# Keys and values of a cross attention by seven products of halved blocks instead of eight

## The chip, the cores and the metric

The kernel runs on one core of a Trainium2 chip. Its metric is the device time of one execution in microseconds (us). The matrix engine is TensorE (PE); VectorE (DVE), ScalarE (ACT) and GpSimd (POOL) work beside it, and SyncE (SP) issues most of the transfers. All arithmetic here is in 32-bit floating point.

## The reference, cut to what matters

Two decoder layers work on 8 entries of 256 tokens of width 256. The change lies in the cross attention of the second layer, 16 heads of 64 with one learned key and value ("null") in front. The context of an entry is 256 tokens of width 512:

```
q = split_heads(x @ Wq)                        # [256, 256] @ [256, 1024]
k, v = split(context @ Wkv)                    # [256, 512] @ [512, 2 x 1024]
k, v = concat(null_k, k), concat(null_v, v)
out = softmax(q k^T / 8) v @ Wout              # heads joined, [256, 1024] @ [1024, 256]
x = x + layernorm(out) * ln_scale + ln_bias
```

A feed-forward layer with a shared expert (weights ws1, ws3, ws2) and eight routed experts follows.

## The kernel before

The tiles live in pools; a pool with `bufs=n` gives a name n buffers in turn, and a new use waits until the old one is read. A scheduler orders the instructions of each engine at build time, except where a manual order is declared; each engine then works its own queue from front to back, waiting for semaphores. PE is in manual order in the last entry of the cross attention and after it.

`product` (L272 to L274) is the matmul helper of nearly everything here: it gives one product as two matmuls, one for each 64 columns of the 128 stationary columns. The profile lists each 32-bit matmul as two records, each with its own weight load, so `product` shows as four records.

`null_cross_attention` (L1043) handles the entries b = 0 to 7 in turn. The loop body begins with `weighted(kT, v, qT)` of entry b, which makes the scores (stx, L1100), their exponentials (pTx, ACT, L1104), a sum of the two key halves (both, POOL, L1106), the products with the values (ox, L1138) and, by a matmul with a table of ones, the denominators (den, L1114). Scores of two pairs of heads run ahead; both has four buffers. Then come the layer norm of entry b+1 (`layernorm_T`, transposes tr), the norm and routing scores of entry b-1 for the expert layer (`routed_norm`, `routed_rows`, `routed_scores`: xne, sc), and `reciprocals`, which turns the denominators round, sends them to memory and reads them back spread over partitions (rd, rs). While that transfer is under way PE makes the keys and values of entry b+1:

- `keys(b + 1)` loads the transposed context (ctxT, two buffers) and calls `features` with the key half of wkv_x: 4 groups of 16 matmuls with 256 moving columns (fm, 64 matmuls), each group copied out of the accumulation banks by ACT;
- `vals(ctxT)` makes the values: 4 groups of 8 matmuls with 512 moving columns (vps), each copied by ACT.

After that `divide` multiplies the output by rs (L1186; half on DVE, half on POOL), `outward(b, ...)` multiplies by Wout (wo) and normalizes the result with DVE and POOL (lxrs L256, yx L1203 and L1204, x L1205), and `queries(xnT)` makes the scores of the null key (nps) and the queries of entry b+1 (fm with wq_x, 32 matmuls, four copies on DVE). Then the next entry's `weighted` begins.

The accumulation banks: pool mm has three banks in turn for fm, vps, ox, wo, tr, sc and nps; pool scp has two tiles of two banks for the scores; den has its own. Tag pT has four buffers.

`load_shared` (L920) loads the router and the three matrices of the shared expert once, before the loop, into a pool of their own (L914). In the last entry `wproj.close()` frees the context weights, and the pool "mids" takes their place.

Of the kernel before, what the change touches and what calls it, by code (L numbers as in the profile page):

```python
# [28 lines left out]
F32 = mybir.dt.float32  # L29
# [4 lines left out]
ALU = mybir.AluOpType  # L34
# [4 lines left out]
P = 128  # L39
B, S, D = 8, 256, 256  # L40
# [3 lines left out]
CTX = 512  # L44
XH, XD = 16, 64
# [4 lines left out]
NFC = len(FCH)  # L50
# [105 lines left out]
def plain(  # L156
# [4 lines left out]
    nc = tc.nc  # L161
# [100 lines left out]
    def layernorm_T(b, work, mm):  # L262

        xn = work.tile([P, 2, D], F32, tag="xn", name="xn")
        mv, rs = norm_stats([x[:, 2 * b + t, :] for t in range(2)], 1e-5, small, "ln")
        for t in range(2):
            last = normed(xn[:, t, :], x[:, 2 * b + t, :], mv, rs, t)
        return last, transposed(xn, work, mm, "xnT")
# [3 lines left out]
    def product(out, lhsT, rhs, start, stop):  # L272
        for h in (slice(0, 64), slice(64, P)):
            nc.tensor.matmul(out[h], lhsT[:, h], rhs, start=start, stop=stop, skip_group_check=True)  # L274
# [481 lines left out]
    nc8 = XH // 2  # L756
# [139 lines left out]
    def w_in(pool, src1, src3, name):  # L896

        t = pool.tile([P, 2, 2 * FF + tail], F32, name=name, tag=name)
        nc.sync.dma_start(t[:, :, :FF], src1.rearrange("(c p) f -> p c f", p=P))
        nc.sync.dma_start(t[:, :, FF + tail :], src3.rearrange("(c p) f -> p c f", p=P))  # L900
        nc.gpsimd.tensor_copy(t[:, :, FF : FF + tail], t[:, :, 2 * FF :])
        return t

    def ended(t):

        nc.gpsimd.memset(t[tail:, full, :], 0.0)
        return t

    def w_out(t, src):
        nc.sync.dma_start(t[:, :full, :], src[: full * P].rearrange("(c p) d -> p c d", p=P))  # L910
        nc.sync.dma_start(t[:tail, full, :], src[full * P :])
        return t
# [4 lines left out]
    norms = [(const.tile([P, 2, 2], F32, name=f"mean{b}"), const.tile([P, 2], F32, name=f"rstd{b}")) for b in range(B)]  # L917
    shared = {}

    def load_shared():  # L920

        router = pool_s.tile([P, 2, E], F32, name="router")
        nc.gpsimd.dma_start(router, a["L1_ffn_router_DE"].rearrange("(c p) e -> p c e", p=P))
        xnT = pool_s.tile([P, 2, B * S], F32, name="xnTe")
        ws13 = w_in(pool_s, a["L1_ffn_ws1_DF"], a["L1_ffn_ws3_DF"], "ws13")
        ws2 = w_out(ended(pool_s.tile([P, NFC, D], F32, name="ws2")), a["L1_ffn_ws2_FD"])
        shared.update(router=router, xnT=xnT, ws13=ws13, ws2=ws2)

    def hidden(mid, first, n, pair, silu):

# [109 lines left out]

    def null_cross_attention(phase):  # L1043
        work = phase.enter_context(tc.tile_pool(name="d2", bufs=2))
        scale = XD**-0.5

        def features(dst, w, rows, copy):
            n = w.shape[1]
            for c2 in range(0, nc8, 2):
                ps = mm.tile([P, 2, S], F32, tag="mm", name="fm")  # L1050
                for i in range(2):
                    for cc in range(n):
                        product(
                            ps[:, i, :], w[:, cc, (c2 + i) * P : (c2 + i + 1) * P], rows[:, cc, :], cc == 0, cc == n - 1
                        )
                copy(dst[:, c2 : c2 + 2, :], ps)

        def keys(b):
            ctxT = ctxs.tile([P, CTX // P, S], F32, tag="ctxT", name="ctxT")
            nc.sync.dma_start(ctxT, a["ctx_T"][b].rearrange("(c p) t -> p c t", p=P))  # L1060
            kT = work.tile([P, nc8, S], F32, tag="kT", name="kTx", bufs=1)
            features(kT, wkv_x, ctxT, nc.scalar.copy)
            return ctxT, kT

        def vals(ctxT):
            v = work.tile([P, 2, XH, XD], F32, tag="vx", name="vx", bufs=1)
# [13 lines left out]
            return v  # L1080

        def queries(xnT):
            nps = mm.tile([P, 2, S], F32, tag="mm", name="nps")
            for k in range(2):
                product(nps[:, 0, :], wn[:, k].rearrange("p g w -> p (g w)"), xnT[:, k, :], k == 0, k == 1)
            qT = work.tile([P, nc8, S], F32, tag="qT", name="qTx", bufs=1)
            features(qT, wq_x, xnT, nc.vector.tensor_copy)
            en = work.tile([P, S], F32, tag="en", name="en")
            nc.scalar.activation(en, nps[:, 0, :], AF.Exp, scale=scale)
            return qT, en  # L1090

        def weighted(kT, v, qT):

# [57 lines left out]

        def reciprocals(b, den, en):

            r = work.tile([P, S], F32, tag="rx", name="rx")
            nc.vector.tensor_tensor(r, den, en, ALU.add)
            nc.vector.reciprocal(r, r)
            rd = dram.tile([2, nc8, S], F32, name=f"rd{b}")
            rs = work.tile([P, nc8, S], F32, tag="rs", name="rs", bufs=1)
            for g in range(2):
                nc.sync.dma_start(rd[g], r[XD * g : XD * g + nc8, :])  # L1160
            for g in range(2):
                nc.sync.dma_start(
                    rs[XD * g : XD * (g + 1)].rearrange("p c q -> p (c q)"),
                    rd[g : g + 1].rearrange("g c q -> g (c q)").to_broadcast([XD, nc8 * S]),
                )
            nc.gpsimd.tensor_tensor(en, en, r, ALU.mult)
            low = work.tile([P, S], F32, tag="low", name="low")
            nc.vector.tensor_scalar(low, r, 1.0e-25, None, ALU.is_ge)
            nc.vector.scalar_tensor_tensor(
                low, r, 1.0e25, low, ALU.is_le, ALU.mult, accum_out=fit[:, b : b + 1]  # L1170
            )
            return rs

        def in_range():

            for k in range(3):
                v = dens[:, k].rearrange("p t h -> p (t h)")
                low = work.tile([P, S], F32, tag="low", name="lowk")
                nc.vector.tensor_scalar(low, v, 1.0e-25, None, ALU.is_ge)
                nc.vector.scalar_tensor_tensor(  # L1180
                    low, v, 1.0e25, low, ALU.is_le, ALU.mult, accum_out=fit[:, B + k : B + k + 1]
                )
# [5 lines left out]
                )  # L1188

        def outward(b, oT, en):  # L1190
            y = work.tile([P, 2, D], F32, tag="y", name="yx")
            ps = mm.tile([P, 2, D], F32, tag="mm", name="wo")
            for t in range(2):
                cols = bass.ts(t, P)
                product(ps[:, t, :], en[:, cols], nvw, True, False)
                for c in range(nc8):
                    product(ps[:, t, :], oT[:, c, cols], wout_x[:, c, :], False, c == nc8 - 1)
            nc.scalar.copy(y, ps)  # L1198
            mv, rs = norm_stats([y[:, t, :] for t in range(2)], 1e-6, small, "lx")
            for t in range(2):  # L1200
                xt = x[:, 2 * b + t, :]
                normed(y[:, t, :], y[:, t, :], mv, rs, t)
                nc.gpsimd.tensor_tensor(y[:, t, :], y[:, t, :], lns, ALU.mult)  # L1203
                nc.gpsimd.tensor_tensor(y[:, t, :], y[:, t, :], lnb, ALU.add)  # L1204
                nc.gpsimd.tensor_tensor(xt, xt, y[:, t, :], ALU.add)  # L1205
# [10 lines left out]


        _, xnT = layernorm_T(0, work, mm)
        ctxT, kT = keys(0)
        v = vals(ctxT)  # L1220
        qT, en = queries(xnT)
        load_shared()
        order = ExitStack()
        for b in range(B):
            more = b + 1 < B
            oT, den = weighted(kT, v, qT)
            if more:
                _, xnT = layernorm_T(b + 1, work, mm)
            else:

                wproj.close()
                late = ctx.enter_context(tc.tile_pool(name="mids", bufs=1, side="right"))

                shared["mid_s"] = [ended(late.tile([P, NFC, 2 * S], F32, name=f"mid{i}")) for i in range(2)]
                routing_tables(late)
                order.enter_context(tc.manual_schedule(engines={mybir.EngineType.PE}))
            if b:
                routed_rows(b - 1, routed_norm(b - 1, work), work)
            rs, old = reciprocals(b, den, en), en
            if b == 1:  # L1240
                in_range()
            if more:
                ctxT, kT = keys(b + 1)
            if more:
                if b:
                    routed_scores(b - 1)
                v = vals(ctxT)
            else:
                for i, _ in enumerate(quarter(0)):
                    if i == 0:  # L1250
                        routed_scores(b - 1)
            divide(oT, rs)
            outward(b, oT, old)
            if more:
                qT, en = queries(xnT)
        order.close()
        with tc.manual_schedule(engines={mybir.EngineType.PE, mybir.EngineType.DVE}):
            for i, _ in enumerate(quarter(1)):
# [1228 lines left out]
```

## Time and profile before

| | |
|---|---|
| median of 3 runs | 1399.54 us (1398.04 to 1402.86) |
| profiled execution, its own time | 1396.5 us |
| its span | 1394.8 us |
| granted TensorE clock | 0.994 of full speed |
| PE busy | 1357.5 us, 97% of the span |
| keys of eight entries, fm<-ctxT,wkv_x | 112.9 us, 1024 records of 256 columns |
| values of eight entries, vps<-wkv_x,ctxT | 111.8 us, 512 records of 512 columns |
| queries of eight entries, fm<-xnT,wq_x | 57.0 us, 512 records |
| wo<-wout_x,oT | 58.0 us, 512 records |
| POOL both (L1106) | 79.6 us, 64 of 1273 ns |

Busy time of a group is the union of its records, so it is what the group takes of PE, while the mean length of one record includes its overlap with its neighbours. The span is the time between the first and last instruction that the profiler saw; the execution's own time is 1.7 us longer. In a timeline the columns are start (us from the start of the span), length, engine, source line, operation, tiles, shapes and count, and in brackets the idle time before it with what ended it.

### The profile page before, as it was taken

Reading aid. Unit: us, or ns where it says so; the run is one execution under the profiler, and the core shown is the slowest. Engines: PE = TensorE matmul, PEld = TensorE weight load, DVE = VectorE, ACT = ScalarE, POOL = GpSimd, SP = SyncE. Lnnn points to the kernel's source line nnn. Section 1 sums busy time; section 2 is a strip of 40 time slices with the busy share of each in tenths; the row PEclk is TensorE's granted clock in tenths of the full one; section 3 lists DMA queues with packets and bytes.
Section 4 is the critical chain, followed back from the end, with each engine's and each line's share of the span. In section 5 each row is a group of like instructions: output and inputs, shape, how many; then the busy total and the mean of one; then the engine's idle time right before and its main releaser. Section 6 shows DMA issues by size and latency. Waiting matters only on the chain.

```text
span 1394.8 us, 28640 instructions
## 1 busy us (share of the span) xinstructions
PE 1357.5 (97%) x12198; PEld 884.4 (63%) x12198; DVE 502.4 (36%) x1467; ACT 457.4 (33%) x730; POOL 395.7 (28%) x499
## 2 busy tenths in 40 slices
PE   6999999999999999989999999999999999999998
PEld 3666756756766666665655656565656555688884
DVE  5443563563565654330222213131312225422213
ACT  2555444444444434431222313131322222122221
POOL 4222142052033234220332415152423412400004
PEclk9999999999999999999999999999999999999999
DMA  8960000000000006010101010110101010779954
GB/s 312 345 205 16 9 24 9 8 24 1 1 9 2 2 9 221 1 53 26 32 16 31 16 47 2 46 32 16 32 1 32 1 31 5 283 289 414 402 209 127
DMA packets 46921, 116.56 MB, mean 84 GB/s; under 512 B 8273, under 2 KB 30401, under 8 KB 42433
## 3 DMA queue, kind: packets, MB, share of 16 engines
q1 hardware_dynamic: 38912, 92.74, 19.3%
q0 software_dynamic: 5152, 18.89, 3.6%
q10 hardware_dynamic: 2720, 3.02, 0.6%
q8 instruction: 98, 1.61, 0.5%
q14 instruction: 39, 0.31, 0.1%
HBM read 104.00 MB, written 27.93 MB: 95 GB/s over the span
## 4 chain that ended last, share of the span: by engine, by line
PE 85%; DVE 5%; POOL 4%; issue 1%; ACT 1%; DMA 0%; ACTq 0%; POOLq 0%; DVEq 0%; SPq 0%
PE fm L274 12%; PE st L332 9%; PE o L364 9%; PE vps L274 8%; PE h L274 6%; PE wo L274 4%; PE ox L1138 4%; PE stx L1100 4%; PE out L1475 3%; PE out L1292 3%; PE h L947 3%; PE qk L274 3%; PE hx L947 3%; PE tr L281 3%; PE den L1114 2%; PE ao L274 2%
## 5 line engine op out<-in xcount | busy, mean ns | idle before, releaser
L364 PE MATMUL o<-pT,padv 128*64 128x256 f32 (+1 forms) x1536 | 171.6, 365 | 1.1 <-POOL pT L344 1.1
L341 ACT ACTIVATE pT<-st 128x1024 f32<-128x1024 f32 (+1 forms) x128 | 110.5, 915 | 88.8 <-PE st L332 87.9
L364 PEld LDWEIGHTS o<-pT,padv 128*64 128x64 f32 x1536 | 103.1, 137 | 52.7 <-issue 10.0
L332 PE MATMUL st<-qm,kT 64*128 64x256 f32 (+1 forms) x1024 | 117.2, 367 | 0.9 <-DVE qm L310 0.6
L274 PE MATMUL fm<-ctxT,wkv_x 128*64 128x256 f32 x1024 | 112.9, 380 | 0.0
L274 PE MATMUL vps<-wkv_x,ctxT 128*64 128x512 f32 x512 | 111.8, 593 | 0.0
L332 PEld LDWEIGHTS st<-qm,kT 64*128 64x128 f32 x1024 | 90.1, 189 | 26.0 <-issue 15.6
L274 PEld LDWEIGHTS fm<-ctxT,wkv_x 128*64 128x64 f32 x1024 | 73.0, 137 | 37.3 <-issue 1.3
L1106 POOL TENSOR_TENSOR both<-pTx 128x512 f32<-128x512 f32 x64 | 79.6, 1273 | 57.4 <-ACT pTx L1104 33.8
L1104 ACT ACTIVATE pTx<-stx 128x1024 f32<-128x1024 f32 x64 | 62.1, 1021 | 89.9 <-PE stx L1100 86.8
L274 PE MATMUL h<-xrT,w 128*64 128x128 f32 (+1 forms) x1936 | 86.9, 250 | 1.4 <-issue 1.4
L274 PEld LDWEIGHTS h<-xrT,w 128*64 128x64 f32 x1936 | 84.3, 137 | 4.4 <-issue 2.1
L274 PEld LDWEIGHTS vps<-wkv_x,ctxT 128*64 128x64 f32 x512 | 36.4, 137 | 68.9 <-issue 68.6
L341 ACT ACTIVATE pT<-st,kbias 128x1024 f32<-128x1024 f32 x64 | 68.0, 1113 | 28.7 <-PE st L332 28.7
L256 POOL TENSOR_TENSOR lnrs<-lnve,mhalf 128x2 f32<-128x2 f32 x48 | 34.2, 717 | 147.0 <-DVE lnve L254 95.2
L332 PE MATMUL st<-qm,memk 64*128 64x256 f32 x512 | 68.8, 393 | 0.5
L939 ACT ACTIVATE sl<-h 128x128 f32<-128x128 f32 (+1 forms) x114 | 35.4, 310 | 96.1 <-PE h L274 56.7
L1100 PE MATMUL stx<-qTx,kTx 64*128 64x256 f32 x512 | 64.3, 391 | 2.5 <-ACT pTx L1104 2.5
L940 DVE TENSOR_TENSOR midr<-sl,h 128x128 f32<-128x128 f32 x102 | 29.4, 288 | 100.5 <-PE h L274 68.6
L251 DVE BATCH_NORM_STATS2 lxst<-yx 128x6 f32<-128x256 f32 x16 | 6.0, 418 | 162.7 <-ACT yx L1198 162.7
L274 PE MATMUL qk<-l_wqkv,xnT 128*64 128x512 f32 x256 | 62.6, 610 | 0.7 <-ACT xnT L284 0.7
L344 POOL TENSOR_SCALAR_AFFINE_SELECT pT<-pT 128x512 f32<-128x512 f32 x64 | 39.5, 638 | 83.1 <-ACT pT L341 79.8
(274 smaller groups left out, 2080.7 us busy)
## 6 DMA issues: line engine op xcount, KB each, us to landing
w<-packs SPq DMA_DIRECT2D x22, 1408.0 KB
w<-packs SPq DMA_DIRECT2D x22, 768.0 KB
rs<-rd SPq DMA_DIRECT2D x16, 512.0 KB
packs<-L_ffn_w_eDF SPq DMA_DIRECT2D x8, 704.0 KB
packs<-L_ffn_w_eDF SPq DMA_DIRECT2D x8, 640.0 KB
packs<-L_ffn_w_eFD SPq DMA_DIRECT2D x8, 640.0 KB
ctxT<-ctx_T SPq DMA_DIRECT2D x8, 512.0 KB
wkv_x<-L_xattn_Wkv POOLq DMA_DIRECT2D x1, 4096.0 KB, 17.3
```

The costliest lines, as they stand in the source:

```text
L274: nc.tensor.matmul(out[h], lhsT[:, h], rhs, start=start, stop=stop, skip_group_check=True)
L281: nc.tensor.transpose(ps[:, c, t * P : (t + 1) * P], rows[:, t, c * P : (c + 1) * P], ident)
L332: nc.tensor.matmul(st[:, g, i, :n], kT[rows, c, bass.ts(kt, P)], qm[rows, 2 * mq + i, c, q0:], start=True, stop=True,)
L341: nc.scalar.activation(pT[:, :, :, :n], st[:, :, :, :n], AF.Exp, scale=scale, **kb)
L364: nc.tensor.matmul(o[64 * i : 64 * i + 64, mq, q0:], v_pad[:, kt, 4 * c + 2 * mq + i, 2 * g : 2 * g + 2, :], pTs[kt][:, g, i, : S - q0], s ...
L947: nc.tensor.matmul(h, shared["ws13"][:, c, lo : lo + P], shared["xnT"][:, c, bass.ts(q, 2 * S)], start=c == 0, stop=c == 1)
L1100: nc.tensor.matmul(st[:, g, kt, :], kT[rows, c, bass.ts(kt, P)], qT[rows, c, :], start=True, stop=True)
L1104: nc.scalar.activation(pT, st, AF.Exp, scale=scale)
L1106: nc.gpsimd.tensor_tensor(both, pT[:, :, 0, :], pT[:, :, 1, :], ALU.add)
L1138: nc.tensor.matmul(o[XD * g : XD * (g + 1), i, :], v[:, kt, 2 * (c2 + i) + g, :], pT[:, g, kt, :], start=kt == 0, stop=kt == 1, skip_group ...
L1292: nc.tensor.matmul(ps, mid[:, i, lo : lo + P], w2[:, i, :], start=i == 0, stop=i == NFC - 1)
L1475: nc.tensor.matmul(ps[h], mid[:, i, h], sets[k % len(sets)][1][:, i, :], start=i == 0, stop=i == NFC - 1, skip_group_check=True,)
```

## The change

For entries 1 to 7 keys and values are made by the seven products of the Strassen-Winograd scheme. The product context times weights is cut into blocks: the tokens into two halves of 128, the 512 context features into two of 256, and the output columns into two of 512, for the keys and the values each. Four sums of weight blocks are made once (three in a new tile tw, the fourth in place of block (0, 1)); four sums of context blocks are made for every entry on DVE (three in sw, one in place). `seven` issues the products, the accumulating sums and the evacuations, and is a generator, so that keys and values alternate and a bank is read while PE fills another. Each product of the keys is 16 matmuls of 128 moving columns, each of the values 4 of 512. Entry 0 is made as before.

The queries of entry b+1 are moved ahead of `divide` and `outward` of entry b and are interleaved with the last products of the values. The null key's exponential follows its scores at once. The context is requested at the start of the loop body. To make room, the three matrices of the shared expert are loaded in the last entry, when the context weights are given up, and the tiles rx, low and y have one buffer instead of two.

```diff
-    def load_shared():
-        router = ...
-        ws13 = w_in(pool_s, a["L1_ffn_ws1_DF"], a["L1_ffn_ws3_DF"], "ws13")
-        ws2 = w_out(ended(pool_s.tile([P, NFC, D], F32, name="ws2")), a["L1_ffn_ws2_FD"])
+    def load_router():
...
+    def load_shared(pool):
+        shared["ws13"] = w_in(pool, a["L1_ffn_ws1_DF"], a["L1_ffn_ws3_DF"], "ws13")
+        shared["mid_s"] = [ended(pool.tile([P, NFC, 2 * S], F32, name=f"mid{i}")) for i in range(2)]
+        shared["ws2"] = ended(pool.tile([P, NFC, D], F32, name="ws2"))
...
+        tw = wsum.tile([P, 3, half, 2, XH * XD // 2], F32, name="tw")
+        t1, t2, t3, t4 = tw[:, 0], tw[:, 1], w_block(0, 1), tw[:, 2]
...
+            for m in range(2):
+                for c in range(half):
+                    nc.vector.tensor_tensor(dst[:, c, m], p[:, c, m], q[:, c, m], ALU.subtract)
...
+            nc.vector.tensor_tensor(s1, block(1, 0), block(1, 1), ALU.add)
+            nc.vector.tensor_tensor(s2, s1, block(0, 0), ALU.subtract)
+            nc.vector.tensor_tensor(s4, block(0, 1), s2, ALU.subtract)
+            nc.vector.tensor_tensor(s3, block(0, 0), block(1, 0), ALU.subtract)
...
+            xy = scp.tile([P, 2, 2 * S], F32, tag="sc", name=f"kv{m}")
+            xb, yb = xy[:, 0], xy[:, 1]
+            def product_of(n, bank, fresh):
+                s, t = terms[n - 1], w_terms[n - 1][:, :, m, :]
+                for i in range(4 if m == 0 else 1):
+                    for c in range(half):
+                        if m == 0:
+                            args = bank[:, bass.ts(i, P)], t[:, c, bass.ts(i, P)], s[:, c, :]
+                        else:
+                            args = bank, s[:, c, :], t[:, c, :]
+                        product(*args, fresh and i == 0 and c == 0, c == half - 1)
...
+            def kept(bank, name):
+                t = work.tile([P, 2 * S], F32, tag="pT", name=f"kv{name}{m}", bufs=4)
+                nc.scalar.copy(t, bank)
+                return seen(t)
+            product_of(1, xb, True)
+            p1 = kept(xb, "p")
+            yield
+            zb = mm.tile([P, 2 * S], F32, tag="mm", name=f"kvz{m}")
+            product_of(2, zb, True)
+            nc.vector.tensor_tensor(of(0, 0), p1, seen(zb), ALU.add)
+            product_of(5, yb, True)
+            p5 = kept(yb, "v")
+            yield
+            product_of(6, xb, False)
+            u = kept(xb, "u")
+            yield
+            product_of(7, xb, False)
+            nc.vector.tensor_tensor(of(1, 1), p5, seen(xb), ALU.add)
+            yield
+            product_of(3, yb, False)
+            nc.vector.tensor_tensor(of(0, 1), u, seen(yb), ALU.add)
+            product_of(4, xb, False)
+            nc.scalar.copy(of(1, 0), seen(xb))
+            yield
...
         for b in range(B):
             more = b + 1 < B
+            if more:
+                ctxT = context(b + 1)
             oT, den = weighted(kT, v, qT)
             if more:
                 _, xnT = layernorm_T(b + 1, work, mm)
+                terms = sums_of_context(ctxT)
             else:
                 wproj.close()
...
+                load_shared(late)
                 routing_tables(late)
...
             rs, old = reciprocals(b, den, en), en
...
+            if not more:
+                w_out(shared["ws2"], a["L1_ffn_ws2_FD"])
             if more:
-                ctxT, kT = keys(b + 1)
-            if more:
+                k7, v7, q = seven(terms, 0, kT), seven(terms, 1, v), queries(xnT)
+                for made in (k7, k7, k7, v7, k7, v7, k7, v7):
+                    next(made)
                 if b:
                     routed_scores(b - 1)
-                v = vals(ctxT)
+                next(q)
+                next(v7)
+                next(q)
+                next(v7)
+                qT, en = next(q)
...
             divide(oT, rs)
             outward(b, oT, old)
-            if more:
-                qT, en = queries(xnT)
```

## The prediction

> **What bounds the kernel now.** I read the busy table and the chain that ended last first, to learn which engine counts at all.
>
> ```profile
> span 1394.8 us, 28640 instructions
> PE 1357.5 (97%) x12198; PEld 884.4 (63%) x12198; DVE 502.4 (36%) x1467; ACT 457.4 (33%) x730; POOL 395.7 (28%) x499
> ...
> PE 85%; DVE 5%; POOL 4%; issue 1%; ACT 1%; DMA 0%; ACTq 0%; POOLq 0%; DVEq 0%; SPq 0%
> ```
>
> TensorE (PE) is the path. An average over stages doesn't say what one stage is worth, so I then asked for the chain in order of time over the cross attention with heads of 64. It repeats every 63.7 us; one entry, with the start of the next:
>
> ```profile
> 721.65 1.09 PE stx L1100 x8
> ...
> 729.75 1.01 PE den L1114 x8
> ...
> 739.75 0.86 PE den L1114 x8
> ...
> 741.64 13.96 PE fm L274 x128
> 755.60 0.42 PE sc L274 x16
> 756.02 13.78 PE vps L274 x64
> 769.80 7.77 PE wo L274 x72
> 777.57 0.86 PE nps L274 x8
> 778.43 6.91 PE fm L274 x64
> 785.34 1.09 PE stx L1100 x8
> ```
>
> Start, length, piece. Each piece begins where the last ended: keys (fm x128), values (vps), outward (wo), queries (nps, fm x64), then the next entry's scores. Between 640 and 1180 us the waits of PE name one recurring line:
>
> ```profile
> PE stx L1100 <- ACT pTx L1104: 2.5, 8, 0.3
> ```
>
> 2.5 us in eight entries: whatever leaves PE here shortens the kernel, and a new wait lengthens it at full price.
>
> **What the Trainium skill says.** (1) "TensorE: Matmul & The Clock Gate", Back-to-back issue gap, gives a stream of weight load and matmul pairs about 81 ns each at 128 moving columns, while the matmul alone would take 56: narrow products may be bound by their weight loads. This trace disagrees (below: 56 ns). (2) The same page's table of specifications says that VectorE, ScalarE and GpSimd work their queues strictly in order. The trace shows POOL in one such order, below; so the place of an instruction in a queue matters as much as its length. (3) "SBUF — State Buffer", SBUF: two separate sides: a VectorE operation with two SBUF inputs and a GpSimd operation that reads SBUF exclude each other. The trace agrees: the divisions at L1186, which run on both at once, take 678 to 1770 ns on DVE.
>
> **The change, part by part.** A record count is twice the matmul count here (one key stage is 64 matmuls, 128 records).
>
> *Keys.* Removed: 128 records of 256 columns, 13.96 us. Added: 7 products of 16 matmuls, 224 records of 128 columns. The nearest row is the expert stage, whose helper, 64-column weights and 128 moving columns are the same:
>
> ```profile
> 1229.64 4.95 PE h L274 x88
> ```
>
> 4.95/88 = 56.2 ns, so 224 x 56.2 = 12.60 us: 1.36 saved. The weight load could be the floor, but the 64-column form of that row runs 880 records in 26.8 us (30 ns), so it lies well under 56. Bounds: half of the present 109 ns gives 54.5 ns, 12.21 us (1.75 saved); the page's 81 ns gives 18.1 us (4.2 lost). I take 56.2, since it is measured in this kernel.
>
> *Values.* 64 records of 512 columns become 56 of the same: 13.78/8 = 1.72 us saved.
>
> Together 3.08 us an entry, seven entries: **-21.6 us**.
>
> *Evacuations.* Before: 8 ACT copies (586 ns). After: 8 ACT copies, 6 DVE additions (one PSUM operand; I use the 690 ns of a 128x512 copy or product from PSUM), 4 additions of 128x256 for the context (some 0.4 us each): 5.8 us more DVE in an entry where DVE works under 17 of 64 us. Off the path if no bank is awaited. Product 7 overwrites the bank that ACT copies after product 6; three value matmuls (6 records, 1.3 us) lie between for the keys, and scores and null key, 0.86 to 1.3 us, for the values, against a 0.59 us copy. Covered; without that cover a copy costs about 0.65 us each, twice an entry. The built order puts the DVE division, which waits for the reciprocals' DMA, between these additions. That DMA lands some 10 us after the key stage begins (688.7 against 678.4 in the first entry), and the first addition behind it is due after 12; the next PE use of those banks comes later still. No cost. The context sums of the entry after next stand ahead of three query copies: 1.7 us, while the third feature bank gives PE over 1.7 us. No cost.
>
> *Sums of weights.* 16 DVE operations of 128x512, once, 0.65 to 1.2 us each. Twelve run beside entry 0's 27 us of keys and values. Four must wait for its last read of the block and stand ahead of the query copies: 2.7 us, when the first copy was due 2.8 us after the values ended. Taken as zero, at most 2 us once.
>
> *Shared expert weights, loaded late.* Their two 704 KB loads now wait until entry 7's queries release the space. Before, they were issued at 621.3 and 621.7 and ended POOL's wait at 627.5: 6 us. Behind them on SP stand only ws2 and entry 7's reciprocals. PE first reads them some 29 us later. But on POOL the copy that waits for them, with the memsets, now stands ahead of outward(6)'s normalization, which is ready about 9.6 us after those queries end; 4 us of small operations and the 6 us load run side by side. Zero, at most 3 us once.
>
> *Queries moved ahead of outward.* This is the dear part, and no matmul changes. Today 7.77 us of queries lie between the end of wo and the next scores. POOL uses them:
>
> ```profile
> 715.80 0.72 POOL L256 TENSOR_TENSOR lxrs<-lxve,mhalf 128x2 f32<-128x2 f32 x1 [23.58 <-DVE lxve L254]
> ...
> 720.01 0.73 POOL L1204 TENSOR_TENSOR yx<-yx,lnb 128x256 f32<-128x256 f32 x1
> 720.83 0.73 POOL L1205 TENSOR_TENSOR x<-x,yx 128x256 f32<-128x256 f32 x1
> ...
> 724.85 4.95 POOL L1106 TENSOR_TENSOR both<-pTx 128x512 f32<-128x512 f32 x4
> ```
>
> The wo ended at 713.88; the normalization leaves POOL at 721.56, just as scores begin. In the changed program scores begin at once after wo, and POOL's built order is: the chain up to the second lnb, first sum "both", last x, second "both", then mean, two lnrs, rstd, then the other six. Counted from the end of wo: lnb ends at 6.86 (720.74 - 713.88), the first both at 8.1 (4.95/4 = 1.24 each), x at 8.8, the second both at 10.05. PE wants the first two sums at 8.1 (729.75 - 721.65) and 8.6. So the second den waits **1.45 us**. Behind it in PE's queue stand the values of the next heads and all later scores. After that PE and POOL run level: the last sum is ready at about 19.4, PE wants it at 20.0. Seven transitions: **+10.2 us**. Bounds: 0.8 us each if the two sums overlap more than the records show, 2.5 if POOL is slowed by VectorE and the later sums come late too. The gain by which wo itself no longer precedes the queries is nothing, since PE waits for neither.
>
> **Sum:** -21.6 + 10.2 = -11.4 us on the profiled execution, 1396.5 us with what lies around its span, so 1385.1. That execution is 3.0 us under the median of 1399.54; on the median the same step gives **1388**.
>
> **The rivals.** *POOL does not hold PE:* the sums come in time, 7 x 3.08 to 7 x 3.47 us are kept, 1375 to 1378. For it: POOL's records are rough. Against: the count above uses only their starts. *POOL holds PE longer:* at 2.1 to 3.1 us a transition the gain goes to almost nothing, 1393 to 1400; 3.08 us is the point where it turns. *Weight loads bind the narrow key products:* beyond 56.2 + 1.63/0.224 = 63.5 ns a record the change loses; at 71 ns, the busy PEld time per load at fm (73.0 us/1024), keys cost 16.0 us and an entry is slower by 1.7 us, 1412; at the page's 81 ns, 1427. Against it speaks the expert row. *The change doesn't do what it says:* excluded by the built order, which has seven products of 16 and of 4 matmuls in each of seven entries.
>
> **Chances.** Main case (stall 0.8 to 2.1 us) 0.52; POOL in time 0.20; POOL longer 0.16; weight loads or another new wait that loses 0.12. About 4.2 us (0.3%) is what a measurement can tell from no change. Of the third case a third still counts as faster; so faster 0.77, same 0.11, slower 0.12. Range 1375 to 1400: it holds the first three cases nearly whole.
>
> **What would show it.** In the chain after: fm and vps of seven entries replaced by kv pieces of about 1.8 us (32 records) and 1.72 us (8 records), no PE wait on ACT or DVE at L274; PE waiting about 1.5 us on POOL both at den in each of seven entries, none in the first; entry period near 62 us. It is wrong if 32 key records take over 2.0 us, if den never waits, or if PE waits for sw, kv copies or the late ws.

## The result, and the profile after

The changed kernel is **slower**: 1405.49 us median (1404.31 to 1408.27, six runs) against 1398.79 us (1397.67 to 1402.86, six runs), a ratio of 1.0048 with an interval of 1.0030 to 1.0065. The prediction was 1388 us, so 17.5 us are missing. The profiled execution took 1406.25 us with a span of 1404.5 at a granted clock of 0.994, as before.

From the page of after: the span, and the busy table (engine, us, share, instructions).

```profile
span 1404.5 us, 30000 instructions
PE 1353.2 (96%) x12814; PEld 920.4 (66%) x12814; DVE 554.4 (39%) x1553; ACT 457.9 (33%) x730; POOL 388.1 (28%) x499
```

PE's busy time fell by 4.3 us where the products alone should have saved 21.6. So the loss is of two kinds: PE stands idle for longer, and it is busy for longer than its work asks. For the first, the waits of PE between 640 and 1190 us of after (who waits, for whom, us in total, times, longest):

```profile
PE den L1231 <- POOL both L1223: 8.8, 7, 1.3
PE stx L1217 <- ACT pTx L1221: 2.5, 8, 0.3
PE kv L274 <- DVE kTx L1172: 2.1, 7, 0.3
```

The first line is the predicted one, the second stood there before, the third was not predicted. For the second kind, the timeline of PE in after, one entry with the start of the next entry's attention:

```profile
744.99 1.92 PE L274 MATMUL kvz<-ctxT,wkv_x 128*64 128x128 f32 x32
746.74 1.92 PE L274 MATMUL kv<-sw,tw 128*64 128x128 f32 x32
748.48 1.02 PE L274 MATMUL kv<-wkv_x,ctxT 128*64 128x512 f32 x2
749.39 1.97 PE L274 MATMUL kv<-sw,tw 128*64 128x128 f32 x32
751.19 1.46 PE L274 MATMUL kv<-wkv_x,ctxT 128*64 128x512 f32 x5
...
760.79 1.97 PE L274 MATMUL kv<-ctxT,tw 128*64 128x128 f32 x32 [0.30 <-DVE kTx L1172]
...
770.62 1.03 PE L274 MATMUL fm<-xnT,wq_x 128*64 128x256 f32 x6
771.74 1.94 PE L274 MATMUL kv<-tw,ctxT 128*64 128x512 f32 x8
...
777.83 0.38 PE L274 MATMUL wo<-nvw,en 128*64 128x256 f32 x1
777.83 0.38 PE L274 MATMUL fm<-xnT,wq_x 128*64 128x256 f32 x1
...
794.31 0.65 PE L1231 MATMUL den<-both,hot 128*64 128x256 f32 x4
796.22 0.65 PE L1231 MATMUL den<-both,hot 128*64 128x256 f32 x4 [1.26 <-POOL both L1223]
```

A whole key product (x32) moves the start of the next by 1.75 us (746.74 - 744.99), 54.7 ns a record: a little better than the 56.2 taken. A whole value product takes 1.72 for 8 records (in e6 below, 748.67 - 746.95). But the first value product is in two pieces: two records, which are one half-matmul on 64 columns, ahead of keys' product 6, and six behind it. The lone half takes 0.91 us (749.39 - 748.48) where two half-matmuls side by side take 0.86. A second value product, the values' product 6, is parted in the same way round keys' product 4, and the queries by 3 and 21 half-matmuls round the values' product 4 (771.74). At 777.83 the halves are still out of step: a record of wo runs beside one of fm. These partings are in PE's built queue.

PE's list above names one wait among them, but it counts idle time from the modelled end of a matmul, and a lone half that still counts as busy hides that the other 64 columns have no work. The list of the weight loads (PEld), in the same window, names three waits at the products, in each of seven entries:

```profile
PEld kv L274 <- DVE kTx L1172: 7.2, 7, 1.0
PEld kv L274 <- ACT kvv L1153: 5.4, 7, 0.8
PEld kv L274 <- DVE vx L1172: 3.7, 7, 0.6
```

They stand at keys' product 4 (760.79), keys' product 6 (749.39) and the values' product 4 (771.74): at the product right behind each lone half. Each of these three products writes one bank of a two-bank tile, and starts 0.05 us after ACT or DVE has finished reading the other bank.

The groups of after show it too (busy us, mean ns; idle before). Both did the same work before in 57.0 and 58.0 us:

```profile
L274 PE MATMUL fm<-xnT,wq_x 128*64 128x256 f32 x512 | 63.4, 379 | 0.0
L274 PE MATMUL wo<-wout_x,oT 128*64 128x256 f32 x512 | 62.8, 379 | 0.0
```

Those busy times are unions, and each group now shares part of its time with its neighbour, so they point at the fault and do not price it. The page's chain cannot price it either, as it breaks off in after.

The price comes from the period. From one second key product to the next (744.99 to 809.47) it is 64.48 us; before it was 63.69 (two starts of scores, 785.34 - 721.65). So an entry is 0.79 us longer where 1.63 shorter was predicted; seven of them are 5.5 us of the 6.7 between the medians.

### The profile page after: what moved, and what is told of

Read it like the earlier page. It is cut to its first block, busy times and chain, and to the rows that moved or that the text cites. A ratio compares the mean times of both kernels' runs of the same rounds, so it can differ in the third digit from the quotient of the medians.

```text
span 1404.5 us, 30000 instructions
## 1 busy us (share of the span) xinstructions
PE 1353.2 (96%) x12814; PEld 920.4 (66%) x12814; DVE 554.4 (39%) x1553; ACT 457.9 (33%) x730; POOL 388.1 (28%) x499
## 5 line engine op out<-in xcount | busy, mean ns | idle before, releaser
L274 PE MATMUL fm<-xnT,wq_x 128*64 128x256 f32 x512 | 63.4, 379 | 0.0
L256 POOL TENSOR_TENSOR lxrs<-lxve,mhalf 128x2 f32<-128x2 f32 x8 | 5.6, 704 | 207.9 <-DVE lxve L254 207.9
L274 PE MATMUL wo<-wout_x,oT 128*64 128x256 f32 x512 | 62.8, 379 | 0.0
L1255 PE MATMUL ox<-pTx,vx 128*64 128x256 f32 x512 | 61.1, 381 | 0.0
L1217 PEld LDWEIGHTS stx<-qTx,kTx 64*128 64x128 f32 x512 | 46.1, 186 | 20.3 <-issue 9.2
```

Of the source, the lines that this page charges most:

```text
L256: nc.gpsimd.tensor_tensor(rs[:, :n], ve[:, :n], mhalf[:, :n], ALU.pow)
L1217: nc.tensor.matmul(st[:, g, kt, :], kT[rows, c, bass.ts(kt, P)], qT[rows, c, :], start=True, stop=True)
L1255: nc.tensor.matmul(o[XD * g : XD * (g + 1), i, :], v[:, kt, 2 * (c2 + i) + g, :], pT[:, g, kt, :], start=kt == 0, stop=kt == 1, skip_group ...
```

## The experiments

**Theory A:** the products and POOL cost what the prediction says, and the rest was lost because halves of a product were parted in PE's queue and because PE writes a bank of a two-bank tile while the other bank is still read. **Rival B:** the order of the products is harmless, and what is missing lies in POOL, in DVE or in the late shared weights. Ratios below are to the kernel before, timed on the same chip in the same session; periods are read between the same instructions of two entries.

**e1: halves kept together.** PE is put in manual order in this stage; keys' products 3 and 4 are separated.

```diff
+            yield          # between product 3 and product 4
...
-                for made in (k7, k7, k7, v7, k7, v7, k7, v7):
-                    next(made)
+                with tc.manual_schedule(engines={mybir.EngineType.PE}):
+                    for made in (k7, k7, k7, v7, k7, v7, k7, v7, k7):
+                        next(made)
...
+                    for made in (q, v7, q, v7, q, v7):
+                        next(made)
```

> The changed kernel with one edit: PE's order in the key and value stage is written by hand, so that the two 64-column halves of every product stay next to each other (the built order had put 1 + 3 matmuls of a value product, or 3 + 21 of the queries, around other products); the keys' products 3 and 4 no longer stand together. Theory A (halves that are parted no longer run side by side): an entry's 64.5 us fall by the 2.7 us that no wait explains and by the 0.3 us wait at the keys' product 4, so seven entries give about -20 us: 1385. The den wait on POOL stays at 1.3 us. Theory B (products of 128 columns, or the changes of width and bank, cost more than the expert row says): only the waits move, 1403.

Measured: 1394.74 us, ratio 0.9969 (0.9958 to 0.9979), period 62.92. The order alone turns slower into faster, 1.56 us an entry against after. That speaks against B, but half of A's gain is missing too. The new order also takes away the wait at keys' product 4, so this run does not separate the two parts of A. The waits of e1 say where it is:

```profile
PE den L1232 <- POOL both L1224: 8.8, 7, 1.3
PE kv L274 <- ACT kvv L1153: 5.2, 7, 0.7
```

In my order keys' product 6 follows product 5 at once. It writes xb, and ACT is still copying yb, the other bank of the same tile xy: PE idles 0.74 us.

**e3: e1, with three of the four query groups behind outward.**

```diff
-                    for made in (q, v7, q, v7, q, v7):
+                for made in (q, v7, q, v7, v7):
...
             outward(b, oT, old)
+            if more:
+                *_, (qT, en) = q
```

> As e1, and three of the four query groups are put behind the product with Wout again. Theory A with the POOL wait as second cause: the seven den waits (8.8 us in all) go, and nothing takes their place: 1385 - 9 = 1376. If the den waits are hidden by something that is late next, 1383 to 1386. Theory B: 1394.

Measured: 1392.74 us, ratio 0.9955 (0.9942 to 0.9967), period 62.42. A miss for the larger numbers. The wait of den fell from 8.8 to 3.0 us and did not go: POOL's root for the next layer norm (lnrs) waited in its queue for DVE's lnve, ahead of the sums. A new wait of 1.1 us for DVE vx came at the values' product 4, behind two score matmuls that had slipped in ahead of it; some 0.35 us an entry were lost there. It shows only that the queries matter to POOL.

**e4: the kernel before, with the queries moved and nothing else.**

```diff
-            divide(oT, rs)
-            outward(b, oT, old)
             if more:
                 qT, en = queries(xnT)
+            divide(oT, rs)
+            outward(b, oT, old)
```

> The kernel before with one part of the change alone: queries are made ahead of the division and of the product with Wout; keys and values stay as they were. If POOL's order is what makes den wait, den waits 1.3 us in each of seven entries: 1399 + 9 = 1408. If that wait comes from the seven products or their copies, 1399.

Measured: 1412.16 us, ratio 1.0092 (1.0078 to 1.0105), 12.5 us over before (1399.62 there). Without any of the seven products the wait is the same as in after, to the tenth:

```profile
PE den L1114 <- POOL both L1106: 8.8, 7, 1.3
```

The period is 65.26 us, 1.57 longer than before, so the move of the queries costs 11 us in seven entries by itself, and the step that priced it at 10.2 stands. The rest is not explained.

**e5: e1, with one value product parted again** (product 1, one half-matmul ahead of keys' product 6 and three behind it).

> As e1, with one split put back: the first product of the values is issued as 1 matmul ahead of the keys' product 6 and 3 matmuls behind it. Theory A, by column groups that each work in order: the lone 512-column matmul holds its half for 0.86 us while the other half stands idle for 0.43, and behind the three about 0.32 more are lost: 0.75 us an entry, 5 us in all above e1. Theory B: the same time as e1.

Measured: 1393.73 us, ratio 0.9960 (0.9948 to 0.9973), period 62.91 as in e1. The parting costs nothing here. The lone half of 0.91 us stands where e1 waited 0.74 for ACT, and PE's list no longer names that wait; but it is not gone, as the weight loads show:

```profile
PEld kv L274 <- ACT kvv L1153: 5.4, 7, 0.8
```

From keys' product 5 to product 6 e1 takes 2.66 us (745.63 to 748.29) and e5 2.66 (746.49 to 749.15). Half a product laid into the wait neither shortens nor lengthens it. The next order has no such wait.

**e6: whole products, and no bank written beside a reader.** Between two uses of the tile of one operand there is now a product of the other. The cut is against e1.

```diff
-                    for made in (k7, k7, k7, v7, k7, v7, k7, v7, k7):
+                    for made in (k7, k7, v7, k7, v7, k7, v7, k7, v7, k7, v7):
...
-                    for made in (q, v7, q, v7, q, v7):
-                        next(made)
-                    qT, en = next(q)
+                    next(q)
+                    next(q)
+                    next(v7)
+                    *_, (qT, en) = q
```

> As e1 (halves of a product never parted), with the products put in an order in which PE never writes a bank while another engine still reads the other bank of the same tile: keys 1, 2+5, values 1, keys 6, values 2+5, values 6, keys 7, values 7, keys 3, keys 4, values 3, scores, null key, eight query records' matmuls, values 4, the other queries, then outward. In e1 PE waited 0.74 us (0.9 with what follows it) in front of keys' product 6. Theory A (parted halves and waits for banks are what the sum left out): e1 less 7 x 0.9 = 6 us, about 1388, with the wait of den for POOL's both (1.3 us, 7 times) as the only large wait left. Rival B (the order of the products does not matter, e1's gain was chance): 1395, as e1.

Measured: **1386.08 us**, ratio 0.9920 (0.9906 to 0.9934), period 61.96. PE's timeline in e6, some of the products and the two den:

```profile
745.21 1.92 PE L274 MATMUL kv<-sw,tw 128*64 128x128 f32 x32
746.95 1.89 PE L274 MATMUL kv<-wkv_x,ctxT 128*64 128x512 f32 x8
748.67 1.92 PE L274 MATMUL kv<-sw,tw 128*64 128x128 f32 x32
...
790.26 0.65 PE L1232 MATMUL den<-both,hot 128*64 128x256 f32 x4
792.17 0.65 PE L1232 MATMUL den<-both,hot 128*64 128x256 f32 x4 [1.26 <-POOL both L1224]
```

Among the products nothing waits and nothing is parted. This is the kernel that the prediction described, and it comes within 2 us of the predicted 1388. The instructions are those of after; their order on PE is worth about 18 us.

**e8: e6, with the queries behind outward again.** The edit is that of e3, for all four groups, with the null key's scores left in front.

> As e6, with the query products behind outward (as in the kernel before) and the null key's scores left where e6 has them. Theory A (den waits because outward's normalization now runs beside the next scores): the wait at den goes, e6 less 7 x 1.3 to 1.5 = about 1378, period of an entry about 60.5 us. Rival (POOL is late for another reason, or another wait takes the place): as e6, 1388.

Measured: **1375.12 us**, ratio 0.9840 (0.9826 to 0.9853), period 60.33. The waits of PE in e8 between 640 and 1190 us begin with the old line, and den is not among them:

```profile
PE stx L1218 <- ACT pTx L1222: 2.1, 8, 0.3
```

**e10: e6, with four of outward's operations on DVE instead of POOL**; the queries stay ahead.

```diff
-                nc.gpsimd.tensor_tensor(y[:, t, :], y[:, t, :], lns, ALU.mult)
-                nc.gpsimd.tensor_tensor(y[:, t, :], y[:, t, :], lnb, ALU.add)
+                nc.vector.tensor_tensor(y[:, t, :], y[:, t, :], lns, ALU.mult)
+                nc.vector.tensor_tensor(y[:, t, :], y[:, t, :], lnb, ALU.add)
```

> As e6, queries still ahead of outward, but the two multiplications and additions of outward's normalization with ln_scale and ln_bias (L1203, L1204 of the kernel before) run on DVE instead of POOL: four operations of 0.7 us leave POOL's queue ahead of the first sums both. Theory A (POOL's queue holds den): the wait at den goes, about 1378. Rival (the wait is for wo itself or DVE is as late): den still waits, 1388, or DVE's stx copies come late and it is over 1388.

Measured: 1375.21 us, ratio 0.9842 (0.9828 to 0.9855), period 60.33. Two edits that have nothing in common but POOL's queue ahead of the sums take away the same wait and the same time. That settles POOL as its cause.

**e9: e6, with one value product parted**, meant as the clean form of e5.

```diff
-            product_of(1, xb, True)
+                for j in range(4):
+                    c, h = j // 2, slice(64 * (j % 2), 64 * (j % 2) + 64)
+                    nc.tensor.matmul(
+                        xb[h], s[:, c, h], t[:, c, :], start=c == 0, stop=c == half - 1, skip_group_check=True
+                    )
+                    if j == 0:
+                        yield
```

> As e6, but the value product 1 is issued as one half-matmul ahead of keys' product 6 and three behind it, as the built order of the changed kernel has it; nothing else. In e5 a wait of e1 vanished at the same time, so that run could not tell. Theory A (the two 64-column halves of a product share PE's time only when they follow each other in its queue): one half-product alone costs 0.43 to 0.9 us, e6 plus 7 x 0.86 = 6 us, about 1394. Rival B (where the halves stand does not matter): as e6.

Measured: 1391.69 us, ratio 0.9961 (0.9947 to 0.9975), period 62.90: 5.6 us over e6 in the same session, 0.94 an entry, as A has it. But the parting also brings back the wait of e1: only half a product now stands between keys' product 5 and product 6. The timeline of e9 (the parted product is at L1162; ACT and PEld for the first microsecond alone):

```profile
746.06 1.02 PE L1162 MATMUL kv<-wkv_x,ctxT 128*64 128x512 f32 x2
746.33 0.59 ACT L1153 COPY kvv<-kv 128x512 f32<-128x512 f32 x1 [2.90 <-PE kv L274]
746.97 0.20 PEld L274 LDWEIGHTS kv<-sw,tw 128*64 128x64 f32 x4 [0.77 <-ACT kvv L1153]
746.97 1.97 PE L274 MATMUL kv<-sw,tw 128*64 128x128 f32 x32
748.76 1.03 PE L1162 MATMUL kv<-wkv_x,ctxT 128*64 128x512 f32 x4
749.62 0.59 PE L274 MATMUL kvz<-wkv_x,ctxT 128*64 128x512 f32 x1
749.63 0.59 PE L1162 MATMUL kv<-wkv_x,ctxT 128*64 128x512 f32 x1
```

From the lone half to product 6 there are again 0.91 us (746.97 - 746.06), and from product 5 to product 6 2.66 (744.31 to 746.97), as in e1, where no half stands between. ACT's copy of the other bank ends at 746.91 and product 6 starts 0.05 us later, so the wait alone would give this start. The half's own two records, 0.43 us each, end at nearly the same time; e9 does not tell the two apart, and so is no proof of a cost of parting. Further on the two halves work side by side on different products, record by record (749.62 and 749.63).

**e11: e6, with the two other partings of the built order** (a value product round keys' product 4, queries 3 and 21 round the values' product 4). The value product here is product 7, which stands at that place in e6; in after it was product 6.

> As e6, with the two other partings that the built order of the changed kernel has: a value product (the seventh) issued as one half-matmul ahead of keys' product 4 and three behind it, and the queries as 3 half-matmuls of their second group ahead of the values' product 4 and the other 21 behind it. Nothing else; no bank is awaited. Theory A (a half that stands alone runs alone, and its partner is then late by it): 0.86 us for the parted values as in e9 and up to 0.43 for the parted queries, 7 x 1.3 = 9 us over e6, about 1395; with e9's 5.6 us that is nearly all by which the changed kernel lies over e6. Rival B (only a parting at keys' product 6 costs, by what stands round it): as e6, 1386.

Measured: 1403.75 us, ratio 1.0022 (1.0015 to 1.0029), period 64.08, that is 2.12 over e6 where A had 1.3. A wait had slipped in, as the values' product 3 now follows product 7 at once (DVE and PEld only as far as they bear on keys' product 4):

```profile
760.11 1.02 PE L1174 MATMUL kv<-wkv_x,ctxT 128*64 128x512 f32 x2
760.33 0.69 DVE L1182 TENSOR_TENSOR kTx<-kvu,kv 128x512 f32<-128x512 f32 x1 [2.60 <-PE kv L274]
761.07 0.31 PEld L274 LDWEIGHTS kv<-ctxT,tw 128*64 128x64 f32 x6 [0.82 <-DVE kTx L1182]
761.07 1.97 PE L274 MATMUL kv<-ctxT,tw 128*64 128x128 f32 x32
762.87 1.89 PE L1174 MATMUL kv<-wkv_x,ctxT 128*64 128x512 f32 x6
765.61 1.94 PE L274 MATMUL kv<-wkv_x,sw 128*64 128x512 f32 x8 [0.85 <-DVE vx L1179]
```

From the start of the parted product to product 3 there are 5.50 us; the same two products take 3.46 in e6 (762.52 - 759.06). Both places have a wait: keys' product 4 starts 0.05 us after DVE's addition has read the other bank (761.02), 0.96 us behind the lone half, and product 3 waits as in e12 below, where that costs 1.03. Together they are 1.99 of the 2.04 between the two runs, so here too nothing is left for the parting itself. From there to outward e11 takes 11.72 us and e6 11.67: the parted queries cost 0.05 us, so A's term for them was too high. At this parting nothing is awaited, as DVE's addition ended at 768.28, and a record of the next product starts beside the lone half:

```profile
770.43 0.81 PE L1222 MATMUL fm<-xnT,wq_x 128*64 128x256 f32 x5
770.87 0.64 PE L274 MATMUL kv<-tw,ctxT 128*64 128x512 f32 x1
771.08 0.38 PE L1222 MATMUL fm<-xnT,wq_x 128*64 128x256 f32 x1
```

The one parting without a wait behind it is thus the one that costs next to nothing.

**e12: e6, with keys' product 4 right behind product 3**, as in after.

> As e6, but keys' product 4 follows product 3 at once, as in the changed kernel, with no value product between: PE writes one bank of the tile while DVE still reads the other into kTx. Theory A (the wait is for the whole tile, not for the bank): PE waits for DVE kTx, about 0.3 to 0.9 us of idle time in seven entries, 2 to 6 us over e6. Rival B (a wait is for the bank alone, and the changed kernel's 0.3 us had another cause): no wait, as e6.

Measured: 1402.91 us, ratio 1.0016 (1.0009 to 1.0023), period 64.05. More than expected, because the values' product 3 came next to product 7 here too, so there are two such waits. Waits and PE's timeline of e12:

```profile
PE kv L274 <- DVE vx L1169: 6.0, 7, 0.9
PE kv L274 <- DVE kTx L1172: 5.5, 7, 0.8
```

```profile
760.62 1.92 PE L274 MATMUL kv<-sw,wkv_x 128*64 128x128 f32 x32
763.33 1.97 PE L274 MATMUL kv<-ctxT,tw 128*64 128x128 f32 x32 [0.79 <-DVE kTx L1172]
765.12 1.89 PE L274 MATMUL kv<-wkv_x,ctxT 128*64 128x512 f32 x8
767.87 1.94 PE L274 MATMUL kv<-wkv_x,sw 128*64 128x512 f32 x8 [0.86 <-DVE vx L1169]
```

From product 3 to product 4 of the keys there are 2.71 us instead of 1.75, from 7 to 3 of the values 2.75 instead of 1.72: 0.96 and 1.03 lost, together 1.99 of the 2.09 by which the period grew. In both places PE writes the bank that nobody reads, and waits for the reader of the other one. The wait is for the tile. Product 2, whose bank is in another tile, does not wait: in e6 it starts at 743.46, while ACT still has to copy product 1's bank (743.73 to 744.32).

## Why the prediction was wrong, point by point

- **Key and value products, 3.08 us saved an entry: right, and a little low.** In e8 no step that PE could feel but these is left, and its period is 63.69 - 60.33 = 3.36 us shorter than before. Seven times that is 23.5 us; the medians differ by 22.5. Weight loads do not bind at 54.7 ns a record. The Trainium skill ("TensorE: Matmul & The Clock Gate", Back-to-back issue gap) gives about 81 ns for each pair of load and matmul in a stream at 128 moving columns. The prediction called that refuted by the trace, which goes too far: 54.7 is a mean over two halves side by side. In e6 their records start 7 ns apart and the next two follow 109 ns after the first, so no run here shows the page's figure or its opposite.
- **The second den waits 1.45 us for POOL: right.** POOL's timeline in after, from the second lnb to the second sum:

```profile
792.30 0.73 POOL L1321 TENSOR_TENSOR yx<-yx,lnb 128x256 f32<-128x256 f32 x1
792.99 1.27 POOL L1223 TENSOR_TENSOR both<-pTx 128x512 f32<-128x512 f32 x1
794.21 0.73 POOL L1322 TENSOR_TENSOR x<-x,yx 128x256 f32<-128x256 f32 x1
794.90 1.26 POOL L1223 TENSOR_TENSOR both<-pTx 128x512 f32<-128x512 f32 x1
```

  The scores began at 786.13, so the sums are ready 8.1 and 10.0 us later, as worked out; den runs at 794.31 and 796.22, 1.91 us apart instead of 0.45, a delay of 1.46. The whole step is e6's period less e10's, 1.63 us, or 11.4 in seven entries (10.2 predicted).
- **"Covered" and "No cost" at the evacuations: this step failed, at three places of every entry.** I looked for cover only where a bank is written again (product 7), and priced a missing cover at about 0.65 us. But a write also waits for the reader of the other bank of its tile. Keys' product 6 writes xb while ACT copies yb, with one half-matmul between; keys' product 4 and the values' product 4 write xb while DVE reads yb, the one behind a half-matmul, the other behind three. What was put at nothing costs 2.52 us an entry (table below); a whole wait costs 0.96 to 1.03 (e1 over e6, e12). The prediction named a wait for these copies as a sign that would prove it wrong.
- **"Values. 64 records of 512 columns become 56 of the same": right for whole products**, which take 1.72 us each in e6. The built order, which I had read for the place of the operations on POOL and DVE, parts two of them. By the traces of after, e9 and e11 the product behind a parted value product starts when the reader of a bank is done. A cost of the parting itself is not shown: e5 parts one beside a wait that is there anyway and loses nothing, and no run parts one without such a wait. What the parting does is leave less cover: half a product stands where e6 has a whole one.
- **"No matmul changes" in the moved queries: right in number.** They are parted round the values' product 4; in e11, with nothing awaited, the same parting costs 0.05 us.
- **Context sums, sums of weights and late shared weights at zero: nothing speaks against it.** No wait of PE on them appears, and e8 and e10, which keep them all, have the whole gain. The profiled stretch behind the last den is 3.4 us longer in after than in before (275.8 against 272.4), but 4.5 longer in e4, where the shared weights are loaded early, and 272.4 to 272.8 in e6, e8 and e10, where they are late. So it is not theirs; its cause stays open.

The miss, put together from the stretches of after and e6, which issue the same matmuls:

| stretch of one entry | after | e6, same work | lost |
|---|---|---|---|
| first key product to the end of the null key's scores, without value products 7 and 3 | 22.27 | 20.47 | 1.80 |
| value products 7, 3, 4 and queries, to the start of outward | 12.37 | 12.06 | 0.31 |
| outward to the first den | 16.48 | 16.07 | 0.41 |
| first den to the next first key product | 13.36 | 13.36 | 0.00 |

The sum is 2.52 us, 17.6 in seven entries, against the 17.5 that the prediction missed. The three waits account for it. By the single records of this entry, the 64 columns that ran out of work stand idle for 0.91 us before keys' product 6 (748.48 to 749.39), 0.94 before keys' product 4 (759.84 to 760.79) and 0.52 before the values' product 4 (771.23 to 771.74), and each restart takes 0.05 us more than later records do. That is 2.37 + 0.15 = 2.52. This is an estimate from the trace of after alone. The rows do not match the waits one by one, since the halves stay out of step from one row to the next. No run declares the two banks as two tiles and leaves the built order as it is, which would settle it.

e8 and e10 beat both kernels: 0.984 of before, and by the two ratios 0.979 of after (0.984/1.0048; 0.977 to 0.982 from the two intervals).

## What to carry to other kernels

Price a built order and not a count. When two accumulation banks are declared as one tile, a write to either waits for the readers of both, so put other work between: a whole product of 1.72 us is enough here, half of one is not. Two tiles should do as well, but that was not run. When a matmul is issued as two half-width ones, look at the waits of the weight loads too, since one busy half hides that the other stands idle; and look in the queue for halves whose partner is elsewhere, because they cover a wait only by half. And when work is moved off the place where it covered another engine's queue, that cover has a price of its own, which can be measured alone by making that move in the old kernel.

## What the runs showed that I had not expected

- A half-matmul laid into a wait is worth nothing. From keys' product 5 to product 6 there are 2.66 us in e1 with nothing between, and 2.66 in e5 and e9 with a half-matmul between, since the free 64 columns wait all the same. The Trainium skill ("TensorE: Matmul & The Clock Gate", Part 3: Packing small matmuls) says that matmuls start and end in the order of the queue and are not reordered. The end of e11's query half differs: a record of the values' product 4 starts at 770.87, ahead of the half's last record at 771.08, which stands before it in the program. So that order does not explain why nothing starts beside the lone halves of after and e9, while the wait can.
- A wait of 0.74 to 0.86 us for a tile's reader costs 0.9 to 1.0 us of PE's time (e1, e12). The Trainium skill ("PSUM — Partial Sum Buffer", PSUM bank collisions raise a hardware error) puts the dependency between engines at one bank and a quarter of its partitions. The waits seen here, 0.30 us in after and 0.79 in e12, are for another bank of the same tile, and a bank in a tile of its own is not awaited (product 2 in e6). So they most likely come from how the program tracks its tiles and not from what that page describes.
